# Layer 1's attention rebuilt: scores of four heads by 32 queries, 32x32 transposes on VectorE, sums on 32-row array tiles

## The chip, the core and the metric

The kernel runs on one core of one Trainium2 chip. Its time is the device time in microseconds (us) of one execution; the median of several is given. PE is TensorE's matmul side and PEld its weight loads, DVE is VectorE, ACT is ScalarE, POOL is GpSimd, SP is the engine that issues most DMAs. fp32 is used throughout; one fp32 matmul call of the program stands as two MATMUL instructions (with two weight loads) in the trace.

## The reference, cut to what matters

The program has four layers on x of shape (2, 256, 32, 32): two attentions over the image (layers 0 and 1), then a windowed attention with a mixture of experts, and an additive attention with a mixture of experts. The change touches layer 1 alone:

```
xn = groupnorm over the whole image (one mean, one variance), * gn_w + gn_b
q, k, v = w_in @ xn            # 8 heads of 64, N = 1024 positions
attn = softmax(q.T @ k / 8)    # per image and head, 1024 x 1024
out = attn @ v                 # 8 heads of 64 -> 512 channels
x = x + w_out @ out + b_out
```

For each of 2 images and 8 heads that is a 1024 x 1024 table of scores: 16 tables in all.

## The kernel before, in words

`run` calls `layer0`, then `layer1`, then turns `xT` (channels on partitions) into tokens, then the later layers. Nothing of the others is changed, but layer 0's `shared_attention` is of use as a source of durations: it makes scores on 64-row, 32-column tiles of the array (L261), turns most of its weights over with DVE transposes in 32x32 blocks (L311) and sums with 128-row, 64-column tiles (L337). Window attention makes its scores on 32-row, 64-column tiles (L752).

`layer1` first takes the statistics (L574 to L580, `pool_stats`, `rsqrt`), then works through 64 steps, written out by hand in `attention` under `manual_schedule`, so each engine runs its instructions in the order of the program. A step is one image, one pair of heads, 128 queries and all 1024 keys:

- `prepare` (only at the start of an image or a pair): `image` normalises on DVE (L594, L598) and makes the values (L607, copied out by ACT L611); `heads` makes this pair's queries and keys (L621, out by ACT L625).
- `score` (L132): four calls, two heads on the two 64-row halves of the array, into two PSUM tiles of 1024 columns. DVE copies each out with its minimum (L138); the scores carry a minus sign.
- `weigh` (L149): ACT's exp with the minimum as bias, and the row total.
- `turn` (L162): 16 transposes on PE into three PSUM buffers `ps_t`, copied out by ACT (L167, three of four) and DVE (L165).
- `invert`, `spread` (L180 to L190): the reciprocal of the total, spread along a row by POOL, turned by PE, copied by ACT.
- `value` (L199): 16 calls of 128 rows, 64 columns of the array; DVE multiplies the sums by the reciprocals into `oT` (L205). After an image's last step `output` (L634) projects and adds to `xT` on DVE (L640).

The stages lag behind each other: in step n PE runs score of n, the spread of n-3, turn of n-2 and the sums of n-3.

Of the kernel before, what the change touches and what calls it, by code (L numbers as in the profile page):

```python
# [27 lines left out]
P = 128  # L28
# [36 lines left out]
class Stack:  # L65
# [34 lines left out]

    def attention(self, rows, keys, pools):

        tc, nc = self.tc, self.nc
        p_s, p_t, p_o, sb = pools
        KB = 1024
        per = keys // KB
        lag = per + 1
        steps = [(i, j) for i in range(len(rows)) for j in range(per)]
        least, total, scores, weights, sums, norm = {}, {}, {}, {}, {}, {}

        def score(i, j):
            row = rows[i]
            if j == 0:
                row["prepare"]()
                least[i] = self.small.tile([P, 2, per], F32, name="least", tag=f"least{per}")
                total[i] = self.small.tile([P, 2, per], F32, name="total", tag=f"total{per}")
            q, k = row["q"](), row["k"](j)
            ps = [p_s.tile([P, KB], F32, name=f"ps_s{r}") for r in range(2)]
            for c in range(KB // CH):
                for r in range(2):  # L130
                    half = slice(64 * r, 64 * r + 64)
                    nc.tensor.matmul(  # L132
                        ps[r][:, c * CH : (c + 1) * CH], lhsT=q[half], rhs=k[half, c * CH : (c + 1) * CH],
                        start=True, stop=True,
                    )
            scores[i, j] = [sb.tile([P, KB], F32, name=f"sc{r}", bufs=lag + 1) for r in range(2)]
            for r in range(2):
                nc.vector.tensor_scalar(  # L138
                    scores[i, j][r], ps[r], 1.0, None, ALU.mult, ALU.min,
                    accum_out=least[i][:, r, j : j + 1],  # L140
                )
            if j == per - 1 and per > 1:
                m = self.small.tile([P, 2], F32, name="least1")
                nc.vector.tensor_reduce(m, least[i], AX.X, ALU.min)
                least[i] = m.unsqueeze(2)

        def weigh(i, j):
            for r in range(2):
                nc.scalar.activation(  # L149
                    scores[i, j][r], scores[i, j][r], AF.Exp, bias=least[i][:, r, 0:1], scale=-1.0,  # L150
                    accum_out=total[i][:, r, j : j + 1],
                )

        def turn(i, j):
            e = scores.pop((i, j))
            weights[i, j] = {}
            for c in range(KB // CH):
                for r in range(2):
                    ps = p_t.tile([P, CH // P, P], F32, name="ps_t")
                    for k in range(CH // P):  # L160
                        at = c * CH + k * P
                        nc.tensor.transpose(ps[:, k, :], e[r][:, at : at + P], self.ident)  # L162
                    w = sb.tile([P, CH // P, P], F32, name="wt", bufs=9)
                    if c == 1 and r == 1:
                        nc.vector.tensor_copy(w, ps)  # L165
                    else:
                        nc.scalar.copy(w, ps)  # L167
                    weights[i, j][r, c] = w

        def invert(i, j):  # L170

            if j < per - 1:
                return
            t = total.pop(i)
            if per > 1:
                d = self.small.tile([P, 2], F32, name="total1")
                nc.vector.tensor_reduce(d, t, AX.X, ALU.add)
                t = d.unsqueeze(2)
            rec = self.small.tile([P, 2, 1], F32, name="rec")
            nc.vector.reciprocal(rec, t)  # L180
            norm[i] = sb.tile([P, 2, 64], F32, name="wide", bufs=2)
            nc.gpsimd.tensor_copy(norm[i], rec.to_broadcast([P, 2, 64]))

        def spread(i, j):
            if j < per - 1:
                return
            ps = p_t.tile([P, CH // P, P], F32, name="ps_t")
            nc.tensor.transpose(ps[:, 0, :], norm[i].rearrange("p a b -> p (a b)"), self.ident)
            norm[i] = sb.tile([P, P], F32, name="norm", bufs=2)
            nc.scalar.copy(norm[i], ps[:, 0, :])  # L190

        def value(i, j):
            row, w = rows[i], weights.pop((i, j))
            if j == 0:
                sums[i] = p_o.tile([P, P], F32, name="ps_o")
            po = sums[i]
            for k in range(KB // P):
                for r in range(2):
                    nc.tensor.matmul(  # L199
                        po[64 * r : 64 * r + 64, :], lhsT=row["v"](r, j * (KB // P) + k),  # L200
                        rhs=w[r, k // (CH // P)][:, k % (CH // P), :],
                        start=(j == 0 and k == 0), stop=(j == per - 1 and k == KB // P - 1),
                    )
            if j == per - 1:
                nc.vector.tensor_tensor(row["o"](), sums.pop(i), norm.pop(i), ALU.mult)  # L205
                row["finish"]()

        with tc.manual_schedule():
            for n in range(len(steps) + lag + 1):
                at = lambda d: steps[n - d] if 0 <= n - d < len(steps) else None  # L210
                for stage, d in (
                    (invert, lag + 1), (score, 0), (spread, lag + 1), (turn, lag), (weigh, lag - 1), (value, lag + 1)
                ):
                    if at(d):
                        stage(*at(d))

    def attention_pools(self, ctx):
        pool = lambda name, bufs: ctx.enter_context(self.tc.tile_pool(name=name, bufs=bufs, space=PSUM))
        sb = ctx.enter_context(self.tc.tile_pool(name="att_sb", bufs=2))
        return pool("p_s", 1), pool("p_t", 3), pool("p_o", 1), sb  # L220
# [332 lines left out]
    def layer1(self, xT):  # L553
        tc, nc = self.tc, self.nc
        HEADS, HID = 8, 512
        with ExitStack() as ctx:
            w = ctx.enter_context(tc.tile_pool(name="l1_w", bufs=1))
            big = ctx.enter_context(tc.tile_pool(name="l1_big", bufs=1))
            qk = ctx.enter_context(tc.tile_pool(name="l1_qk", bufs=2))
# [3 lines left out]

            pools = self.attention_pools(ctx)
            p_r = pools[1]
# [19 lines left out]
            mean, var = self.pool_stats(w, p_r, mv, average, "ps_t")  # L585
            rs = self.rsqrt(var, 1e-5)
# [3 lines left out]
            def image(b):  # L590
                xn[b] = big.tile([P, CC, N], F32, name="xn", bufs=2)
                for c in range(CC):
                    j = c * B + b
                    nc.vector.tensor_scalar(  # L594
                        xn[b][:, c, :], xT[:, c, b * N : (b + 1) * N],
                        mean[:, j : j + 1], rs[:, j : j + 1], ALU.subtract, ALU.mult,
                    )
                    nc.vector.tensor_scalar(  # L598
                        xn[b][:, c, :], xn[b][:, c, :], gn_w[:, c : c + 1], gn_b[:, c : c + 1],
                        ALU.mult, ALU.add,  # L600
                    )
                v[b] = big.tile([P, N // P, HID], F32, name="v", bufs=2)
                oT[b] = big.tile([P, HID // P, N], F32, name="oT", bufs=2)
                for i in range(N // P):
                    ps = p_r.tile([P, HID], F32, name="ps_t")
                    for c in range(CC):
                        nc.tensor.matmul(  # L607
                            ps, lhsT=xn[b][:, c, i * P : (i + 1) * P], rhs=w_in[:, c, 2 * HID :],
                            start=(c == 0), stop=(c == CC - 1),
                        )  # L610
                    nc.scalar.copy(v[b][:, i, :], ps)  # L611

            def heads(b, pair):

                for part, to, scale in ((0, q, -0.125), (1, k, 1.0)):
                    to[b, pair] = qk.tile([P, N], F32, name="qh" if part == 0 else "kh")
                    for t in range(N // CH):
                        ps = p_r.tile([P, CH], F32, name="ps_t")
                        for c in range(CC):
# [22 lines left out]
            def row(b, pair, i):  # L642
                def prepare():
                    if pair == 0 and i == 0:
                        image(b)
                    if i == 0:
                        heads(b, pair)
# [936 lines left out]
```

## Time and profile before

| what | us |
|---|---|
| median of 3 runs (3086.73 to 3088.11) | 3087.94 |
| the profiled execution | 3088.63 |
| its span | 3086.9 |
| layer 0's steps, about | 60 to 1271 |
| layer 1, reciprocal of the deviation to last addition | 1286.8 to 1792.8 |
| first score of layer 1 / last score of layer 1, start | 1311.0 / 1759.1 |
| PE, DVE, ACT, POOL busy in the span | 2854.8, 1876.2, 1988.2, 447.3 |
| mean granted clock of TensorE | 0.962 |

Rows of groups read: line, engine, operation, output<-input, array rows*columns and shapes, count | busy us, mean ns of one | idle time of the engine just before, and what ended most of it. Rows in order of time read: start, duration, engine, line, operation; "x8" are eight instructions merged, whose duration runs from the first start to the last end, and the ends of matmuls are modelled, so the next instruction can start before. Rows by stage read: from:to, length, then busy time and number of instructions of PE, PEld, DVE, ACT, POOL, then the granted clock as a share of full speed, the DMA share and GB/s.

### The profile page before, as it was taken

What the parts mean: (1) busy time and instruction counts of PE and PEld (TensorE: products, weight loads), DVE (VectorE), ACT (ScalarE), POOL (GpSimd) and SP (SyncE); (2) the same over time, 40 slices, a digit from 0 to 9 for tenths busy, and PEclk for the clock granted to TensorE, in tenths of its full rate; (3) what the DMA queues carried; (4) which work ended last, traced back from release to release, by engine and by line L of the source; (5) the groups of instructions that cost most, each with busy time, mean ns of one, the idle gap of its engine ahead of it and who ended that gap; (6) DMA issues with size and microseconds to landing.
All of it is one profiled execution on the core that took longest, in us unless ns stands there. A gap on an engine that the chain in (4) does not pass through costs nothing.

```text
span 3086.9 us, 71663 instructions
## 1 busy us (share of the span) xinstructions
PE 2854.8 (92%) x29414; PEld 1844.6 (60%) x29414; DVE 1876.2 (61%) x3698; ACT 1988.2 (64%) x2977; POOL 447.3 (14%) x576
## 2 busy tenths in 40 slices
PE   7999999999999999899999978699799977997967
PEld 4466566666666666566566745598566633563656
DVE  5998989889898989445345467653422333223343
ACT  1887878788887878366556622121399776986811
POOL 3000000000000000000000023442311112223233
PEclk9999999999999999999999998799899988999988
DMA  3000000000000000000000010344222112222334
GB/s 125 3 3 3 3 3 3 3 3 3 3 3 3 3 3 3 29 1 1 1 1 1 2 26 1 127 141 150 94 77 75 40 33 74 80 75 73 117 109 150
DMA packets 179894, 126.83 MB, mean 41 GB/s; under 512 B 133152, under 2 KB 161456, under 8 KB 175216
## 3 DMA queue, kind: packets, MB, share of 16 engines
q0 software_dynamic: 36864, 85.93, 8.5%
q1 hardware_dynamic: 141264, 35.87, 5.2%
q8 instruction: 231, 3.78, 0.5%
q14 instruction: 95, 0.78, 0.1%
q10 hardware_dynamic: 1440, 0.47, 0.1%
HBM read 181.24 MB, written 29.49 MB: 68 GB/s over the span
## 4 chain that ended last, share of the span: by engine, by line
PE 84%; DVE 5%; issue 3%; DMA 3%; ACT 2%; POOL 2%; another core or an unknown queue 1%; SPq 0%; POOLq 0%; DVEq 0%; ACTq 0%
PE ps_s L261 15%; PE ps_o L337 15%; PE ps_h L1240 8%; PE ps_y L1254 8%; PE ps_e L1391 7%; PE ps_t L319 5%; PE ps_s L132 4%; PE ps_o L199 4%; PE ps_t L162 4%; PE ps_t L621 2%; PE ps_v L1428 2%; PE ps_out L516 1%; PE ps_qk L450 1%; PE ps_t L607 1%
## 5 line engine op out<-in xcount | busy, mean ns | idle before, releaser
L298 ACT ACTIVATE sc<-sc,sa_shift 128x1024 f32<-128x1024 f32 x512 | 585.1, 1148 | 56.7 <-DMA sa_shift<-sa_min 56.5
L1382 ACT ACTIVATE th<-kT,qb 128x1024 f32<-128x1024 f32 x512 | 542.1, 1135 | 114.2 <-PE ps_e L1391 75.3
L261 PE MATMUL ps_s<-kT,qT 64*32 64x512 f32 x8192 | 504.9, 596 | 9.3 <-ACT sc L271 8.9
L337 PE MATMUL ps_o<-wt,v 128*64 128x128 f32 x6144 | 503.2, 276 | 0.0
L337 PEld LDWEIGHTS ps_o<-wt,v 128*64 128x64 f32 x6144 | 442.1, 137 | 42.8 <-issue 42.8
L311 DVE STREAM_TRANSPOSE wt<-sc 128x768 f32<-128x768 f32 x512 | 465.7, 943 | 1.1 <-ACT sc L298 1.1
L271 ACT COPY sc<-ps_s 128x1024 f32<-128x1024 f32 x256 | 257.3, 1005 | 115.1 <-PE ps_s L261 43.2
L1240 PEld LDWEIGHTS ps_h<-xe,ew 128*128 128x128 f32 x2320 | 278.6, 195 | 62.1 <-issue 35.9
L282 DVE TENSOR_REDUCE sa_least<-sc 128x1 f32<-128x1024 f32 x256 | 306.1, 1196 | 2.5 <-ACT sc L271 2.4
L268 DVE TENSOR_SCALAR_CACHE_REDUCE sc<-ps_s 128x1024 f32<-128x1024 f32 x256 | 301.4, 1177 | 5.9 <-PE ps_s L261 5.9
L1240 PE MATMUL ps_h<-xe,ew 128*128 128x128 f32 x2320 | 293.4, 281 | 10.5 <-DVE xe L1219 8.8
L1391 PE MATMUL ps_e<-th,pick 128*32 128x512 f32 x2048 | 284.7, 619 | 19.7 <-DVE ir_half L955 14.2
L1254 PE MATMUL ps_y<-ew,h 128*128 128x256 f32 x1160 | 272.8, 384 | 8.0 <-issue 4.3
L138 DVE TENSOR_SCALAR_CACHE_REDUCE sc<-ps_s 128x1024 f32<-128x1024 f32 x128 | 151.8, 1222 | 180.2 <-PE ps_s L132 180.2
L337 PE MATMUL ps_o<-wl,v_odd 128*64 128x128 f32 x2048 | 251.9, 276 | 0.0
L1254 PEld LDWEIGHTS ps_y<-ew,h 128*128 128x128 f32 x1160 | 212.7, 190 | 64.5 <-issue 21.8
L261 PEld LDWEIGHTS ps_s<-kT,qT 64*32 64x32 f32 x8192 | 127.3, 106 | 200.7 <-issue 170.1
L1229 ACT ACTIVATE h<-hb 128x512 f32<-128x512 f32 x145 | 90.1, 623 | 243.5 <-DVE hb L1245 197.1
L1245 DVE TENSOR_TENSOR hb<-ps_h,ew 128x512 f32<-128x512 f32 x145 | 100.1, 690 | 240.0 <-PE ps_h L1240 202.0
L319 PEld LDWEIGHTS ps_t<-ident,sc 128*128 128x128 f32 x1024 | 107.8, 141 | 216.4 <-issue 172.0
L337 PEld LDWEIGHTS ps_o<-wl,v_odd 128*64 128x64 f32 x2048 | 221.2, 137 | 0.0
L348 POOL TENSOR_TENSOR diag<-ident,sa_rec 32x128 f32<-32x128 f32 x64 | 25.1, 391 | 1172.4 <-DVE sa_rec L345 1172.4
(266 smaller groups left out, 3660.4 us busy)
## 6 DMA issues: line engine op xcount, KB each, us to landing
xr<-slots_in SPq DMA_DIRECT2D x99, 128.0 KB
slots_out<-y SPq DMA_DIRECT2D x99, 128.0 KB
sa_got<-sa_least SPq DMA_DIRECT2D x512, 0.5 KB
sa_shift<-sa_min SPq DMA_DIRECT2D x512, 0.2 KB
slots_in<-zero POOLq DMA_DIRECT2D x46, 128.0 KB
sa_sums<-sa_total SPq DMA_DIRECT2D x256, 1.0 KB
xT<-in_x SPq DMA_DIRECT2D x4, 496.0 KB
ew<-in_l_up,rt_rows POOLq DMA_INDIRECT x99
```

Source lines behind the costliest of these rows:

```text
L261: nc.tensor.matmul(ps[r][S * c : S * (c + 1), a, :].rearrange("p (b i) -> p b i", i=S), lhsT=qT[half, p, S * i : S * (i + 1)], rhs=keys[ha ...
L268: nc.vector.tensor_scalar(scores[m][0], flat[0], 1.0, None, ALU.mult, ALU.min, accum_out=least[m // 2][:, 0, h : h + 1])
L271: nc.scalar.copy(scores[m][1], flat[1])
L282: nc.vector.tensor_reduce(least[m // 2][:, 1, h : h + 1], scores[m][1], AX.X, ALU.min)
L298: nc.scalar.activation(scores[m][r], scores[m][r], AF.Exp, bias=shift[m // 2][:, r : r + 1], scale=-1.0, accum_out=total[i][:, 2 * p + r, ...
L311: nc.vector.transpose(weights[i, h][:, 2 * p + r, :], scores[m][r][:, :DIRECT])
L319: nc.tensor.transpose(ps[:, g, r, :], s[:, at : at + P], self.ident)
L337: nc.tensor.matmul(sums[i][64 * k : 64 * (k + 1)], lhsT=values, rhs=w, start=(h == 0 and j == 0 and t == 0), stop=(h == 1 and j == 1 and t ...
L1240: nc.tensor.matmul(ps[:, j, :], lhsT=a[:, c, at : at + P], rhs=x[:, c, :], start=(c == 0), stop=(c == CC - 1),)
L1254: nc.tensor.matmul(ps, lhsT=h[:, j, :], rhs=w2[:, j, :], start=(j == 0), stop=(j == HB - 1))
L1382: nc.scalar.activation(h, keys, AF.Tanh, bias=self.qb[b][:, s // G, g : g + 1])
L1391: nc.tensor.matmul(pe[i][c * U : (c + 1) * U, a, :], lhsT=self.pick[:, k, :], rhs=h[:, a, :], start=(k == 0), stop=(k == G - 1),)
```

## The change

`attention` and `attention_pools` go; `layer1` gets a schedule of its own with 64 slots in place of the 64 steps:

- A slot (`score`) is four heads by two blocks of 32 queries by 1024 keys: 16 calls on 64-row, 32-column tiles, the four heads on the four column strips, a block of queries on each 64-row half. So that each head meets both halves, every projected query and key tile is stored twice, the second time with its two 64-row halves exchanged by two DMAs (`take` in `heads`).
- DVE copies out with the minimum as before; ACT's exp as before. The reciprocal now scales the weights themselves, on POOL (`share`).
- `turn` is one DVE transpose in 32x32 blocks of each 128 x 1024 tile; nothing goes through PE or PSUM.
- `value`, every second slot: 128 calls with 32 keys of one head (32 rows) by 64 columns, moving 4 x 32 queries; each head has a PSUM bank, the first and second half of the keys go to its lower and upper 64 partitions. `join` copies the upper half out on ACT, and DVE adds the two halves into `oT` (two additions).
- Projections, values and outputs are jobs, two in each odd slot that the table `jobs` names (17 with projections after slot 4, 6 with outputs, within the 64 slots). The values of image 0 are in slots 0 to 3. Jobs and sums share one PSUM buffer of four banks (tag `ps_r`, one buffer); scores have the other four.
- The group norm is folded into one scale and shift; image 1 is normalised on POOL after slot 18.

The diff, without the removed parts that the section above describes and without unchanged setup:

```
-            pools = self.attention_pools(ctx)
-            p_r = pools[1]
+            psum = lambda name: ctx.enter_context(tc.tile_pool(name=name, bufs=1, space=PSUM))
+            p_s, p_r = psum("l1_s"), psum("l1_r")
+            banks = lambda name: p_r.tile([P, H, CH], F32, name=name, tag="ps_r")
...
+            nc.vector.tensor_tensor(by_image(scale), by_image(scale), channel(gn_w), ALU.mult)
+            nc.vector.tensor_tensor(shift, mean, scale, ALU.mult)
+            nc.vector.tensor_tensor(by_image(shift), channel(gn_b), by_image(shift), ALU.subtract)
...
+            def heads(part, b, quad, p, half):
+                def job(ps):
...
+                    for c in range(CC):
+                        nc.tensor.matmul(
+                            ps, lhsT=w_in[:, c, at : at + P], rhs=xn[b][:, c, half * CH : (half + 1) * CH],
+                            start=(c == 0), stop=(c == CC - 1),
+                        )
+                    def take():
+                        nc.scalar.activation(to[:, 0, :], ps, AF.Copy, scale=(-0.125, 1.0)[part])
+                        for r in range(2):
+                            nc.sync.dma_start(
+                                out=to[64 * r : 64 * r + 64, 1, :], in_=to[64 - 64 * r : 128 - 64 * r, 0, :]
+                            )
+                    return take
+                return job
+            def values(b, n):
+                def job(ps):
...
+                    for a in range(4):
+                        at = (4 * n + a) * S
+                        for c in range(CC):
+                            for h in range(H):
+                                nc.tensor.matmul(
+                                    ps[S * h : S * (h + 1), a], lhsT=xn[b][:, c, at : at + S],
+                                    rhs=weights[:, c, h], start=(c == 0), stop=(c == CC - 1),
+                                )
+                    def take():
+                        for u in range(2):
+                            nc.scalar.copy(v[b][u][:, 4 * n : 4 * n + 4, :], ps[:, :, u, :])
+                    return take
+                return job
+            def output(b, n, o):
...
+                    return lambda: nc.vector.scalar_tensor_tensor(
+                        x, ps, b_out[:, o : o + 1], x, ALU.add, ALU.add
+                    )
...
+            jobs = {n: [values(0, 2 * n), values(0, 2 * n + 1)] for n in range(4)}
...
+                5: queries(0, 0, 1), 7: keys(0, 1, 0), 9: keys(0, 1, 1), 11: queries(0, 1, 0), 17: queries(0, 1, 1),
+                21: keys(1, 0, 0), 23: keys(1, 0, 1), 25: queries(1, 0, 0), 35: queries(1, 0, 1), 37: outs(0, 0),
+                39: keys(1, 1, 0), 41: keys(1, 1, 1), 43: outs(0, 1), 45: queries(1, 1, 0), 47: outs(0, 2),
+                49: outs(0, 3), 51: queries(1, 1, 1), 57: outs(1, 0), 61: outs(1, 1), 65: outs(1, 2), 67: outs(1, 3),
+            jobs.update({27 + 2 * n: [values(1, 2 * n), values(1, 2 * n + 1)] for n in range(4)})
+            def score(n):
...
+                            half, side, p = slice(64 * r, 64 * r + 64), (h + r) % 2, h // 2
+                            col = at % CH + S * r
+                                ps[r][S * h : S * (h + 1), a * CH : (a + 1) * CH],
+                                lhsT=x[half, side, p, col : col + S],
+                                rhs=y[half, side, p, a * CH : (a + 1) * CH], start=True, stop=True,
...
+            def weigh(n, r):
+                nc.scalar.activation(
+                    scores[n][r], scores[n][r], AF.Exp, bias=least[n][r], scale=-1.0, accum_out=total[n][r]
+                )
+            def share(n, r):
+                nc.vector.reciprocal(rec[n][r], total[n][r])
+                nc.gpsimd.tensor_scalar(scores[n][r], scores[n][r], rec[n][r], None, ALU.mult)
+            def turn(n, r):
+                if n % 2 == 0 and r == 0:
+                    turned[n // 2] = sb.tile([P, 4, N], F32, name="wt")
+                nc.vector.transpose(turned[n // 2][:, n % 2 * 2 + r, :], scores[n][r])
+            def value(m):
...
+                x, ps = turned.pop(m), banks("ps_o")
+                for t in range(BLOCKS // 2):
+                    for h in range(H):
+                        rows = slice(S * h, S * (h + 1))
+                        for j in range(2):
+                            at = BLOCKS // 2 * j + t
+                            nc.tensor.matmul(
+                                ps[64 * j : 64 * j + 64, h, :P], lhsT=v[b][quad][rows, at, :],
+                                rhs=x[rows, :, S * at : S * (at + 1)], start=(t == 0), stop=(t == BLOCKS // 2 - 1),
+                            )
+            def join(m):
...
+                nc.scalar.copy(other, ps[64:128, :, :P])
+                def add():
+                    for r in range(2):
+                        nc.vector.tensor_tensor(
+                            to[64 * r : 64 * r + 64], ps[0:64, r::2, :P], other[:, r::2, :], ALU.add
                         )
+                return add
+            image(0, nc.vector)
+            with tc.manual_schedule():
+                for n in range(0, len(first), 2):
+                    ps = banks("ps_j")
+                    for take in [job(ps[:, i, :]) for i, job in enumerate(first[n : n + 2])]:
+                        take()
+                for n in range(SLOTS + 4):
+                    on = lambda d: 0 <= n - d < SLOTS
+                    if on(2):
+                        turn(n - 2, 0)
+                    if on(1):
+                        share(n - 1, 1)
+                    if on(2):
+                        turn(n - 2, 1)
+                    copies = score(n) if on(0) else []
+                    add = join((n - 5) // 2) if n % 2 == 1 and on(5) else None
+                    for copy in copies:
+                        copy()
+                    if add:
+                        add()
+                    if on(0):
+                        weigh(n, 0)
+                    takes = []
+                    if n % 2 == 0 and on(4):
+                        value((n - 4) // 2)
+                    elif n in jobs:
+                        ps = banks("ps_j")
+                        takes = [job(ps[:, i, :]) for i, job in enumerate(jobs[n])]
+                        takes.pop(0)()
+                    if on(0):
+                        share(n, 0)
+                        weigh(n, 1)
+                    for take in takes:
+                        take()
+                    if n == NORM:
+                        image(1, nc.gpsimd)
```

## The prediction, on record before the result

> **What bounds the kernel now.** I read the busy times by stage first, then one step of layer 1 in order of time, then the rows elsewhere in this trace that have the shapes the change brings in. Layer 1 runs from the group-norm scale (reciprocal at 1286.8 us) to its last addition into `xT` (ends 1792.8): 506 us of the 3086.9 us span. A steady stretch of it:
>
> ```profile
> core 0: us, PE busy (x) PEld busy (x) DVE busy (x) ACT busy (x) POOL busy (x), PEclk, DMA share, GB/s
> 1400.00:1500.00 100.00, 100.00 (x861) 67.82 (x863) 49.39 (x103) 64.44 (x127) 4.45 (x15) 1.00 0.01 1
> ```
>
> PE has no idle time and full clock; DVE is half empty. One step (two heads, 128 queries, 1024 keys) in order of time:
>
> ```profile
> 1424.42 1.99 PE L132 MATMUL ps_s<-kh,qh 64*128 64x512 f32 x8
> ...
> 1426.34 0.33 PE L188 MATMUL ps_t<-ident,wide 128*128 128x128 f32 x1
> ...
> 1426.44 1.22 DVE L138 TENSOR_SCALAR_CACHE_REDUCE sc<-ps_s 128x1024 f32<-128x1024 f32 x1 [1.47 <-PE ps_s L132]
> 1426.51 1.93 PE L162 MATMUL ps_t<-ident,sc 128*128 128x128 f32 x16
> ...
> 1428.37 1.97 PE L199 MATMUL ps_o<-wt,v 128*64 128x128 f32 x32
> ...
> 1430.26 1.99 PE L132 MATMUL ps_s<-kh,qh 64*128 64x512 f32 x8
> ```
>
> Score to score is 5.84 us, all PE: 1.92 score, 0.17 spread, 1.86 turning, 1.89 sums. 64 steps are 374 us; projections and outputs (per image 15.4 for the values, 4 x 7.06 for heads, 14 out) add 115. First score ends 1313, last 1761.1.
>
> **What the change removes and adds.** Turning and spreading (2.03 x 64 = 130 us of PE) go. DVE gets two 1024-wide transposes per slot, POOL two scalings, ACT loses the PSUM copies. Rows for the new forms:
>
> ```profile
> L311 DVE STREAM_TRANSPOSE wt<-sc 128x768 f32<-128x768 f32 x512 | 465.7, 943 | 1.1 <-ACT sc L298 1.1
> ```
> ```profile
> 699.77 1.95 PE L261 MATMUL ps_s<-kT,qT 64*32 64x512 f32 x32
> 701.64 0.66 PE L319 MATMUL ps_t<-ident,sc 128*128 128x128 f32 x4
> ```
> ```profile
> 1877.26 0.49 PE L752 MATMUL ps_s<-kh,qh 32*64 32x64 f32 x32
> 1877.67 0.33 PE L789 MATMUL ps_pt<-ident,probs 128*128 128x128 f32 x1
> ```
>
> - *Score* is layer 0's form exactly (16 calls, eight 64*32 tiles): 1.87 us to the next instruction, 2.0 to its last result.
> - *Sums*: 128 calls of 32*64 x 128 columns are 256 instructions on eight tiles. A 128-column instruction takes 0.107 us of one tile (L337: 16 rounds in 1.71, 1.90 with the change of form). If the eight overlap, 32 rounds are 3.4, with 0.2 for the change of form **3.6 us** per two slots. L752 shows eight 32*64 tiles overlapping: 32 instructions in 0.41 us, 13 ns each, where 13.4 are needed. Bounds: 3.4, and 6.9 if only four of the eight run together. I take 3.6.
> - The Trainium skill, "TensorE: Matmul & The Clock Gate", Part 1, speaks against this: it says that start to start never drops below about 25 ns however small the matmul is. By it the sums would be 256 x 25 ns = 6.4 us and layer 1 some 90 us longer (an estimate from that page). This trace has 13 ns, so I follow the trace.
> - *DVE*: two copies with minimum 2 x 1.15 (L138, start to start); two transposes of 1024. Pairs of 768 start 0.89 apart, so 1.16 each (between 0.89 and 0.89 x 4/3 = 1.19); two reciprocals 0.13; every second slot two additions of 256 columns, 0.4 each (L816 has 0.42). Even slot 5.15 us, odd 5.95.
> - *POOL*: 128x1024, one input. Nearest rows: L484 copies 512 columns in 0.86, L770 multiplies 512 in 1.04, a 1024 memset is 0.95. So 0.95 to 2.1 each, two per slot, with a whole slot of slack before the transposes: nothing. It would count from 2.7 each.
> - *ACT*: two exps 2.4, one 0.6 copy per two slots, 1.2 to 1.5 for a pair of jobs: under 4.6 per slot, covered.
> - *DMAs*: each of the 32 jobs for heads adds two of 128 KB on SP's queue, which is empty in layer 1 (1 GB/s in the first row above); the slots that read them come three to eleven slots, 17 us or more, later. Nothing but at the start (below). Image 1 is normalised on POOL in slot 18 in two operations of 0.95 to 2.1; first read in slot 21: nothing.
> - *Instructions*: layer 1's PE stream grows some three times; the instruction queue's packets stand at 231 for the whole program. I take nothing; a late packet of 16 KB would cost part of a microsecond.
>
> **The slot.** One PSUM buffer of four banks (`ps_r`) serves sums and jobs in turn, and that sets the order. Let a slot begin when its score's last result is there (T).
> Even slot: sums follow at once, then the next score: 3.6 + 1.87 = **5.5**; DVE's 5.15 fits under it.
> Odd slot without jobs: the next score waits only for the two copies; DVE's 5.95 is late. DVE then carries the pair: with some overlap at the seams 10.8 for two slots.
> Odd slot with jobs (projections): PE stands until DVE has made its two copies (2.3) and both additions (3.1), since the jobs write the banks that the additions read; then two jobs 3.6 (L621: 7.06 for four), then the score 2.0: **8.8**. ACT's second exp waits behind the first job's take, which makes DVE ready at about 8.4: equal, not later.
> Odd slot with outputs: their additions are on DVE, in front of a reciprocal and two transposes: 9.8, less 0.3 regained in the next slot.
> Of the 63 steps from score 0 to score 63: the first five 5.5; then 17 pairs with projection jobs at 14.3, 6 with outputs at 15.0, 6 without at 10.8: 27.5 + 243 + 90 + 65 = **425 us**.
> *Start*: normalising takes DVE 1.6 instead of 3.2 and three small steps more (0.6); PE begins at 1288.6, at half clock until 1292.0 as before; three pairs of projections at 4.4 (one buffer, so the takes are not hidden) end 1303.3. Then the halves of keys and queries are swapped by DMA: 256 KB behind the last takes; the stage 1262 to 1282 moved 77 GB/s at least, so under 3.4 us, plus landing: score 0 ends 1308.5, before 1313.
> *End*: from the last score, sums and outputs alternate through one buffer: 3.2 + 3.6 + 2.1 + 4.1 + 3.6 + 1.8 + 4.1 = 22.5; before, 31.7.
> Sum at full clock: 1308.5 + 425 + 22.5 = 1756, that is **36 us earlier** than 1792.8.
>
> **The clock.** In every odd slot with jobs PE streams nothing for 3.2 us and the 0.15 us that the last score's tail takes: 3.35. Before, layer 1 had no such gap. What such gaps do here is seen in stretches of 3.41 us laid on the instants at which the granted clock changes:
>
> ```profile
> 1254.14:1257.56 3.42, 0.44 (x10) 0.20 (x4) 2.37 (x4) 2.68 (x5) 0.00 (x0) 1.00 0.01 0
> 1257.56:1260.97 3.41, 3.20 (x24) 2.87 (x26) 0.70 (x1) 2.90 (x6) 0.00 (x0) 0.50 0.00 0
> 1520.38:1523.79 3.41, 2.01 (x4) 0.79 (x5) 2.37 (x4) 0.00 (x0) 0.17 (x1) 1.00 0.00 0
> 1523.79:1527.20 3.41, 3.41 (x9) 1.52 (x8) 0.00 (x0) 1.17 (x2) 0.00 (x0) 1.00 0.00 0
> 1882.19:1885.61 3.42, 1.56 (x21) 1.18 (x12) 2.66 (x11) 2.32 (x5) 0.56 (x1) 1.00 0.00 0
> 1885.61:1889.02 3.41, 3.41 (x42) 2.53 (x41) 1.41 (x5) 0.12 (x1) 2.24 (x3) 0.50 0.00 0
> ```
>
> A stretch with PE busy 0.44 or 1.56 us is followed by one at clock 0.50, one with 2.01 is not. So about 2 us idle within a stretch is enough. A gap of 3.35 puts 2 us into some stretch if that begins within 3.35 + 3.41 - 4 = 2.75 of 3.41: 8 gaps in 10. The half-speed stretch then falls on the jobs and the score, which are what the slot waits for: 1.7 us lost, 1.8 with the cases where a second stretch follows. 23 slots x 0.8 x 1.8 = 33; slots after outputs, with gaps a microsecond longer, 3; slots without jobs, where PE has a microsecond in hand, 2; start and end 4. **42 us lost** (bounds: 0, and one stretch in each of 31 odd slots and the ends, 60).
> The same page's rule, § HAM oscillation, that gaps under about 3.4 us are safe would leave nothing of this 42 and give 36 us of gain; the row with 1.56 busy speaks against it.
>
> **Sum.** -36 + 42 = +6 on the profiled execution's 3088.63 (its span 3086.9 and 1.7 around it); the median shown is 0.7 lower, 3087.94. Forecast **3094 us**: the work saved on PE comes back as waiting for the one buffer and as half clock. Own range 3072 to 3116 (clock loss 20 to 64).
>
> **Rivals.**
> 1. *The clock holds*: slots fall so that few stretches have 2 us idle, or half speed falls where DVE is late anyway. For it: 6 of 29 pairs are DVE's. Against: the rows above. 3088 - 36 = **3052** (3040 to 3070).
> 2. *The sums on 32-row tiles do not overlap eightfold* at 128 columns, since each row strip gets 64 weight loads in 3.4 us. L752 is 32 instructions long and shows a burst only. Price: every us beyond 3.6 is paid 32 times, at once in the 23 job pairs. At 4.6 us +32, at 6.9 us +106: 3125 to **3200**. It decides from 3.9 us on.
> 3. *DVE is the bound in every slot* (transposes slower beside POOL): 6.0 per slot only equals today's 5.84, and job pairs have 3 us in hand; +0 to 20, within the forecast's range.
>
> **Chances.** Forecast 0.50, clock holds 0.25, sums slow 0.18, anything else 0.07. Range 3046 to 3145 leaves out part of rivals 1 and 2. This kernel's times can tell 0.2%, 6 us, from no change: faster 0.25 + 0.13 of the forecast's half = 0.38; same 0.14; slower 0.48.
>
> **What would show it.** Sums: groups of 256 matmuls in 3.6 us. Odd job slots: PE idle 3.2 us, ended by DVE's addition. Clock in layer 1 near 0.8 instead of 1.00; if it stays over 0.95, rival 1. Score to score 5.5 and 8.8. Last score near 1773. Wrong if POOL's scaling takes over 2.7 us, or PE waits on transposes.

## The result and the profile after

| what | before | after |
|---|---|---|
| median of 4 runs, us | 3088.03 (3086.73 to 3090.00) | 3173.58 (3168.01 to 3178.53) |
| ratio, 95% interval | | 1.0276 (1.0254 to 1.0298) |
| the profiled execution / its span | 3088.63 / 3086.9 | 3178.53 / 3176.8 |
| mean granted clock of TensorE | 0.962 | 0.945 |
| first result complete / start of last score | 1313 / 1759.1 | 1311.7 / 1848.5 |
| last addition of layer 1 ends | 1792.8 | 1881.1 |
| half clock between 1330 and 1870 us | 15.1, none of it in layer 1 | 112.6 |
| half clock from the first score's result to the last score's end | 13.7 | 109.2 |
| PE instructions in layer 1 / packets of the instruction queue | 7994 / 31 | 23111 / 91 |

Half clock is the time in which TensorE's granted clock stood at 0.50 of full speed.

The change makes the kernel 2.8% slower: 3173.6 against a forecast of 3094 and a range to 3145. Layer 1 ends 88 us later, which is nearly all of the 90 us that the span grew. The line numbers below are those of the changed kernel: score L591, copy with minimum L602, exp L609, scaling on POOL L615, turning on DVE L620, sums L631, other half by ACT L644, additions L648, projection jobs L509, L536 and L553.

The same stage that was read before, by stage, same columns (PE, PEld, DVE, ACT, POOL busy, then the clock):

```profile
1400.00:1500.00 100.00, 72.70 (x1977) 36.65 (x1977) 66.17 (x116) 37.16 (x63) 73.76 (x29) 0.91 0.08 18
```

PE had no idle time and now has 27 us in 100, and its clock is 0.91 where it was 1.00. Where the idle time is, PE's rows in order of time show:

```profile
1405.22 3.67 PE L509 MATMUL ps_j<-xn,sb_l_w_in 128*128 128x512 f32 x8 [3.38 <-DVE oT L648]
1408.82 1.95 PE L591 MATMUL ps_s<-kh,qh 64*32 64x512 f32 x32
1411.19 2.61 PE L631 MATMUL ps_o<-wt,v 32*64 32x128 f32 x163 [0.42 <-ACT qh L515]
1415.21 1.62 PE L631 MATMUL ps_o<-wt,v 32*64 32x128 f32 x93 [1.41 <-issue]
1416.77 1.95 PE L591 MATMUL ps_s<-kh,qh 64*32 64x512 f32 x32
1420.09 3.09 PE L591 MATMUL ps_s<-kh,qh 64*32 64x512 f32 x32 [1.38 <-DVE sc L602]
1423.11 3.48 PE L631 MATMUL ps_o<-wt,v 32*64 32x128 f32 x227
1427.68 0.69 PE L631 MATMUL ps_o<-wt,v 32*64 32x128 f32 x29 [1.08 <-issue]
```

The gap of 3.38 us ahead of the jobs, ended by DVE's addition, is the one that was predicted. The breaks inside the sums (163 and then 93, 227 and then 29) were not: one group of 256 MATMUL instructions runs at 14 ns each, stops once, and goes on. The label "issue" says that PE waited for nothing that the profile shows. The groups of instructions say what it adds up to:

```profile
L631 PE MATMUL ps_o<-wt,v 32*64 32x128 f32 x8192 | 137.1, 275 | 49.6 <-issue 40.4 <-ACT qh L515 3.0 <-ACT v L543 2.8
L509 PE MATMUL ps_j<-xn,sb_l_w_in 128*128 128x512 f32 x128 | 85.2, 828 | 48.0 <-DVE oT L648 39.6 <-DVE l_rec L614 3.5 <-ACT kh L515 2.5
L615 POOL TENSOR_SCALAR sc<-sc,l_rec 128x1024 f32<-128x1024 f32 x128 | 362.6, 2844 | 218.3 <-DVE l_rec L614 218.3
L620 DVE STREAM_TRANSPOSE wt<-sc 128x1024 f32<-128x1024 f32 x128 | 155.3, 1225 | 2.2 <-POOL sc L615 2.2
L489 POOL TENSOR_SCALAR xn<-xT,rs_r,gn_shift 128x1024 f32<-128x1024 f32 x2 | 2.4, 1188 | 0.0
```

A group of sums takes 5.55 us in the mean (3.87 to 7.39), not 3.6. POOL's scaling takes 2.84 us, over the bound of 2.7 that the prediction gave, though a row of the same shape with two operations (L489) takes 1.19; the turning hardly waits for it (2.2 us in all).

The clock, in stretches of 3.41 us laid on its changes, around the gap of slot 5 (score ends at 1343.43):

```profile
1342.28:1345.69 3.41, 1.15 (x24) 0.15 (x8) 2.17 (x3) 0.84 (x1) 3.07 (x2) 1.00 0.00 0
1345.69:1349.10 3.41, 2.30 (x3) 1.18 (x4) 2.26 (x6) 0.40 (x2) 2.16 (x1) 0.50 0.00 0
1349.10:1352.52 3.42, 3.42 (x5) 1.35 (x4) 0.00 (x0) 0.00 (x0) 0.69 (x1) 0.50 0.00 0
```
```profile
1341.48 1.95 PE L591 MATMUL ps_s<-kh,qh 64*32 64x512 f32 x32
1346.80 6.51 PE L509 MATMUL ps_j<-xn,sb_l_w_in 128*128 128x512 f32 x8 [3.37 <-DVE oT L648]
```

PE is idle 2.3 us in the first, and the two that follow, in which the jobs run, stand at half. That slot, from the end of its score to the end of the next, takes 11.8 us; one with no half clock takes 8.9.

**Theories.** Theory A for the stops: PE is out of instructions. The 74480 instructions of PE, its weight loads and its sequencer in this trace come with 291 packets of 16 KB of the instruction queue, that is 256 to a packet. All 30 stops inside the sums lie at the same place of this stream, the first instruction after a whole multiple of 256 (counted from the program's start, less 193), and end 1.25 to 1.60 us after a packet has landed. Three of them, a stop counted from the start of the instruction before it to the start of the next, which is 0.26 us more than the idle time in brackets above:

```
PE stops  multiple of 256 passed before   packet from .. to     PE goes on
1339.02   1337.17                         1337.99 .. 1339.00    1340.39
1413.54   1411.69                         1412.30 .. 1413.75    1415.21
1426.33   1424.50                         1425.32 .. 1426.28    1427.68
```

From one multiple to the next PE needs 2.9 to 4.1 us (median 3.4) where it stops, whereas 256 instructions (128 matmuls with their weight loads) run in 1.8. A group of sums is 512. In the two groups without a stop PE lost about 0.8 us at the same place of the stream in the score that follows. Theory B, the prediction's second rival: the eight 32-row tiles do not overlap over a long group. Theory C for the rest: the gap ahead of the jobs is paid as a wait and again as half clock. Against it: the clock follows the amount of work, or POOL and DVE are next in line and take whatever is freed.

### The profile page after: what moved, and what is told of

The parts are those of the page before. It is cut to its first block, busy times and chain, and to the rows that moved or that the text cites. A ratio compares the mean times of both kernels' runs of the same rounds, so it can differ in the third digit from the quotient of the medians.

```text
span 3176.8 us, 86798 instructions
## 1 busy us (share of the span) xinstructions
PE 2800.2 (88%) x37030; PEld 1777.0 (56%) x37030; DVE 1992.8 (63%) x3831; ACT 1894.6 (60%) x2769; POOL 789.4 (25%) x642
## 5 line engine op out<-in xcount | busy, mean ns | idle before, releaser
L615 POOL TENSOR_SCALAR sc<-sc,l_rec 128x1024 f32<-128x1024 f32 x128 | 362.6, 2844 | 218.3 <-DVE l_rec L614 218.3
L147 DVE TENSOR_SCALAR_CACHE_REDUCE sc<-ps_s 128x1024 f32<-128x1024 f32 x256 | 301.4, 1177 | 6.4 <-PE ps_s L140 6.4
L1418 PE MATMUL ps_e<-th,pick 128*32 128x512 f32 x2048 | 286.3, 628 | 21.6 <-DVE ir_half L982 14.3
L609 ACT ACTIVATE sc<-sc,l_least 128x1024 f32<-128x1024 f32 x128 | 146.8, 1148 | 213.9 <-DVE sc L602 211.3
```

The costliest lines, as they stand in the source:

```text
L147: nc.vector.tensor_scalar(scores[m][0], flat[0], 1.0, None, ALU.mult, ALU.min, accum_out=least[m // 2][:, 0, h : h + 1])
L615: nc.gpsimd.tensor_scalar(scores[n][r], scores[n][r], rec[n][r], None, ALU.mult)
L1418: nc.tensor.matmul(pe[i][c * U : (c + 1) * U, a, :], lhsT=self.pick[:, k, :], rhs=h[:, a, :], start=(k == 0), stop=(k == G - 1),)
```

## The experiments

The runs went to several chips, on which before takes 3062 to 3089 us, so each is compared with before on its own chip. The changed kernel itself, run again:

**after_same_chip.** No edit.

> The changed kernel, unedited, on the chip of the other runs, to compare the single looks with: ratio to before 1.0276 as at first, so about 3147 us where before takes 3062; sums 5.5 us in the mean, stops at every 256 PE instructions, half clock between first and last score 100 to 125 us.

Measured: 3181.4 where before takes 3089.2, ratio 1.0305 (1.0289 to 1.0320); it landed on a chip like the first, so the factor, about 1.029, is what carries over: where before takes 3062, the changed kernel would take about 3151 (worked out, not run). Half clock between 1330 and 1870 us 109 us; pairs of slots with projection jobs 19.07 us where the first trace has 19.04.

**half_rounds.** Leaves out half of the sums.

```diff
-                for t in range(BLOCKS // 2):
+                for t in range(BLOCKS // 4):
...
```

> Leaves out half of the sums: 8 of the 16 rounds of blocks, so 128 matmuls (256 PE instructions with their weight loads) per two slots instead of 256 (512). Theory A, PE is out of instructions in the middle of each group of sums: in the changed kernel every stop lies on a multiple of 256 PE instructions and ends 1.3 to 1.5 us after a packet of the instruction queue has landed; with 256 instructions a group holds one such place, the one for which the packet had time, so the group takes 1.8 to 2.0 us with no stop, at the same 13.4 ns. Theory B, the 32-row tiles do not run together eightfold over a long group: 2.8 us, half of 5.55. The whole run 50 to 90 us below the changed kernel by either; the row decides.

Measured: 3088.3 us (one run; before 3061.9), 63 below the 3151. PE's rows:

```profile
1403.81 2.15 PE L631 MATMUL ps_o<-wt,v 32*64 32x128 f32 x128 [0.42 <-ACT qh L515]
1405.88 2.99 PE L591 MATMUL ps_s<-kh,qh 64*32 64x512 f32 x32
```
```profile
L631 PE MATMUL ps_o<-wt,v 32*64 32x128 f32 x4096 | 69.7, 277 | 9.4 <-ACT qh L515 3.0 <-ACT v L543 2.8 <-ACT kh L515 2.5
```

No stop in any group, and the 40.4 us of "issue" are gone: 2.1 us for 128 matmuls, a little over theory A's 2.0 and well under theory B's 2.8. It also shows that not every us of the sums is paid: 3.4 us less per group, 32 times, is 108, and 63 came back. In an even slot PE then waits for DVE's copies, and job slots without half clock grow from 8.9 to 9.5 us, since DVE is behind when they begin: the gap ahead of the jobs is 3.9 us there, not 3.4.

**narrow_sums.** Leaves out half of the sums in the other direction.

```diff
-                                ps[64 * j : 64 * j + 64, h, :P], lhsT=v[b][quad][rows, at, :],
-                                rhs=x[rows, :, S * at : S * (at + 1)],
+                                ps[64 * j : 64 * j + 64, h, : P // 2], lhsT=v[b][quad][rows, at, :],
+                                rhs=x[rows, 0:2, S * at : S * (at + 1)],
...
```

> Leaves out half of the sums in the other direction: all 256 matmuls (512 PE instructions) per two slots, each over 64 queries instead of 128; the output's other queries are filled with copies. Theory A (instructions): from one multiple of 256 instructions to the next PE needs 3.2 to 3.5 us whatever the matmuls are, so a group takes 3.3 + 0.9 = 4.2 us, its stop grows from 1.6 to about 2.4 us. Theory B (tiles, work by columns): 2.8 us, half of 5.55, with a stop no longer than before. Theory B2 (a price per instruction, no stop): 5.5 us.

Measured: 3169.0 (one run; before 3061.9). A group in order of time:

```profile
1427.85 2.63 PE L631 MATMUL ps_o<-wt,v 32*64 32x64 f32 x227
1432.24 0.48 PE L631 MATMUL ps_o<-wt,v 32*64 32x64 f32 x29 [1.76 <-issue]
```

With half of the columns a group still takes 5.29 us; the stop grows from 1.61 to 2.12 us in the mean, as A has it, and from one multiple of 256 to the next it is 3.6 us in the median, where it was 3.4. So the work is not what the group waits for, which ends theory B. The group's length alone is near B2's 5.5, but B2 has no stop, and between the stops a matmul takes 11 ns. The 4.2 us were a miss: a matmul of 64 columns takes 11 ns and not 7, so the running part shrank by 0.75 us and not by 1.7. Nor is the run shorter than the 3151, for half clock grew from 109 to 178 us between the first and the last score; why was not followed up. The two kernels together: half of the instructions removes the stop, half of the columns does not.

**add_first.** One edit of the order on VectorE.

```diff
-                    for copy in copies:
-                        copy()
                     if add:
                         add()
+                    for copy in copies:
+                        copy()
```

> One edit: in odd slots the additions stand ahead of the two copies on VectorE. Theory C (the gap in front of the jobs brings the half clock): additions end with or before the score, jobs follow the score at once, PE idle ahead of L509 falls from 3.4 us to under 1; half clock in layer 1 falls from 127 us to under 40; job slots go from 8.9 to 11.8 us to 5.6 to 6.5, the 23 pairs with jobs from about 18 to 13.5: the run about 3060 us. Rival (the clock follows the work, not the gap): half clock stays over 100 us and only the wait goes: 3173 - 23 x 3.2 = about 3100. Rival (GpSimd's scaling at 2 x 2.84 per slot, or VectorE, is next in line and takes the gain): over 3120.

Measured: 3043.9 where before takes 3061.9, ratio 0.9928 (0.9904 to 0.9952): the order alone turns 2.8% slower into 0.7% faster. One pair of slots:

```profile
1349.09 3.83 PE L631 MATMUL ps_o<-wt,v 32*64 32x128 f32 x253 [0.42 <-ACT qh L515]
1354.44 0.43 PE L631 MATMUL ps_o<-wt,v 32*64 32x128 f32 x3 [1.52 <-issue]
1354.80 1.95 PE L591 MATMUL ps_s<-kh,qh 64*32 64x512 f32 x32
1356.68 3.70 PE L509 MATMUL ps_j<-xn,sb_l_w_in 128*128 128x512 f32 x8
1360.31 1.95 PE L591 MATMUL ps_s<-kh,qh 64*32 64x512 f32 x32
```

The jobs follow the score at once. ACT copies the other half and DVE adds while the score runs, and the copies, which the jobs do not need, run beside the jobs. Pairs with projections go from 19.04 to 14.04 us, with outputs from 17.97 to 13.29; half clock from the first score's result to the last score's end goes from 109 to 28 us (between 1330 and 1870 us, which here reaches 99 us past layer 1, from 113 to 51; in layer 1 it is 42, a little over the 40 expected). The stop stays.

**add_middle.** The additions between the two copies.

```diff
-                    for copy in copies:
+                    for copy in copies[:1]:
                         copy()
                     if add:
                         add()
+                    for copy in copies[1:]:
+                        copy()
```

> One edit: in odd slots the additions stand between the two copies on VectorE. PE's gap ahead of the jobs falls from 3.4 us to about 2.1. Theory C with the prediction's measure (2 us idle within a stretch of 3.41 us brings the next stretch to half): hardly any job slot is hit, half clock between the first and the last score falls from 113 us to under 40, job slots without half clock 7.8 us, the run about 23 x (1.15 + 1.9) = 70 us below the changed kernel, ratio to before near 1.005. If gaps of 2 us are as bad as gaps of 3.4: half clock stays near 100 us, the run 26 us below.

Measured: 3128.8 (one run; before 3062.8), 23 us below the 3151: the second case, not mine.

```profile
1343.88:1347.29 3.41, 1.18 (x17) 0.30 (x2) 2.49 (x5) 1.21 (x2) 2.84 (x2) 1.00 0.00 0
1347.29:1350.71 3.42, 3.42 (x5) 1.35 (x4) 1.94 (x4) 0.03 (x1) 2.53 (x1) 0.50 0.00 0
```
```profile
1346.89 5.37 PE L509 MATMUL ps_j<-xn,sb_l_w_in 128*128 128x512 f32 x8 [2.23 <-DVE oT L648]
```

A gap of 2.23 us still brings half clock to 20 of the 23 pairs with jobs (106 us in all), only one stretch of it instead of sometimes two. ("Hardly any" did not follow even from the prediction's own formula, by which a gap of 2.1 us puts 2 us into some stretch in 4 cases of 10.) Over the stretches of layer 1 at full clock, in all eleven traces, those with PE busy under 1.3 us were always followed by half, those with 2.15 or more never, and between the outcome was mixed. So idle time of about 1.5 us in a stretch can be enough, where the prediction took 2. In add_first this was:

```profile
1396.80:1400.21 3.41, 1.93 (x26) 0.32 (x18) 2.77 (x7) 1.37 (x3) 2.35 (x1) 1.00 0.03 7
1400.21:1403.62 3.41, 3.41 (x38) 0.78 (x30) 2.55 (x5) 1.02 (x2) 3.24 (x2) 0.50 0.00 0
```

**warm_gap.** Adds work whose result is not used.

```diff
...
+                        if add:
+                            for i in range(26):
+                                nc.tensor.matmul(
+                                    joined[:, 0, CH - P :], lhsT=whole, rhs=whole, start=True, stop=True,
+                                )
                         ps = banks("ps_j")
```

> Adds work: in each odd slot with jobs from slot 5 on, 26 matmuls of 128 columns whose result is not used stand between the score and the jobs, 26 x 0.107 = 2.8 us in a gap of 3.4. The order and the waits stay. Theory C (the gap brings the half clock): half clock in layer 1 falls from 127 us to under 40, job slots go back to 8.9 us, the run is 40 to 55 us shorter, about 3125, though PE does more. Rival (the clock follows the amount of work, or something else than idle time): half clock stays or grows, the run is at 3173 or above.

Measured: 3303.3, ratio to before 1.0790 (1.077 to 1.081), 5% above the changed kernel. It did not test what it was made for:

```profile
1475.22 6.04 PE L683 MATMUL ps_o<-whole 128*128 128x128 f32 x52 [3.37 <-DVE oT L648]
1481.33 3.70 PE L509 MATMUL ps_j<-xn,sb_l_w_in 128*128 128x512 f32 x8
```

The matmuls write a column range that nobody reads, but it lies in the tile that the additions read, and so they waited for the additions as the jobs do; and an fp32 matmul is two instructions, so they last 6.0 us. What it still says: the gap of 3.4 us stands, and so does the half clock, in 20 of the 23 pairs with jobs, with more work on PE; and 25 slots x 6.04 = 151 us were paid in full (152 above the 3151), so in a job slot nothing covers PE.

**pool_forms.** The scaling in four forms, for even and odd slots and the two tiles of a slot.

```diff
...
+ nc.gpsimd.tensor_scalar(scores[n][r], scores[n][r], rec[n][r], zero, ALU.mult, ALU.add)
+ nc.gpsimd.tensor_scalar(to, scores[n][r], rec[n][r], None, ALU.mult)
+ nc.gpsimd.tensor_scalar(to, scores[n][r], rec[n][r], zero, ALU.mult, ALU.add)
```

> GpSimd's 128 scalings in four forms, 32 of each: as in the changed kernel (one operation, in place), two operations in place (times the scalar, plus a zero tile, the form of the normalising row that takes 1.19 us), one operation into another tile, two operations into another tile. If the form makes the 2.84 us against 1.19, the two rows with two operations take 1.2; if being in place makes it, the two rows with another tile do; if sharing with VectorE's work makes it, all four stay near 2.84. Time: theory, GpSimd is off the path (VectorE waits for it 2.2 us in all), so within 0.3% of the changed kernel whatever the rows say; rival, GpSimd at 5.7 us per slot paces the pairs, and a faster form takes 10 us or more off.

Measured: 3138.6 (one run; before 3062.8), 12 us or 0.4% below the 3151. By the marks set beforehand (0.3%, 10 us) that is on the rival's side. But job slots without half clock take 8.93 us as before; what is less is half clock, 72 us against 109 from the first score's result to the last score's end. Whether the form does that one run cannot say; add_first_two_op, below, asks again.

```profile
L618 POOL TENSOR_SCALAR sc<-sc,l_rec 128x1024 f32<-128x1024 f32 x32 | 90.9, 2841 | 105.8 <-DVE l_rec L616 105.8
L623 POOL TENSOR_SCALAR sh<-sc,l_rec 128x1024 f32<-128x1024 f32 x32 | 90.9, 2840 | 127.0 <-DVE l_rec L616 127.0
L627 POOL TENSOR_SCALAR sh<-sc,l_rec,zero 128x1024 f32<-128x1024 f32 x32 | 38.4, 1200 | 69.4 <-DVE l_rec L616 69.4
L620 POOL TENSOR_SCALAR sc<-sc,l_rec,zero 128x1024 f32<-128x1024 f32 x32 | 38.4, 1200 | 0.2 <-POOL sc L618 0.2
```

The form is all of it: with a second operation that does nothing the scaling takes 1.20 us instead of 2.84, in place or not.

**split_sums.** Ten of the 16 rounds of the sums before the next score, six behind it, and the additions between the copies.

```diff
...
                     copies = score(n) if on(0) else []
+                    if n % 2 == 1 and on(5):
+                        value((n - 5) // 2, range(10, 16))
...
-                        value((n - 4) // 2)
+                        value((n - 4) // 2, range(10))
```

> 10 of the 16 rounds of the sums stay in the even slot, 6 come behind the next score, so that a score (64 PE instructions in 1.9 us) stands between 320 and 192 instructions of sums; the additions stand between the two copies. Theory A (a refill each 256 instructions that can't be passed sooner than 3.2 us after the one before): stops shrink from 1.6 us to under 0.5; 2.5 and 1.5 us for the two parts; even slot 4.5, odd slot with jobs 8.7, pairs 13.2 where the changed kernel has 16.8 to 19.8; PE's gap ahead of the jobs 1.4 us, so the clock holds; the run near 3060, ratio to before near 0.99. Theory B (tiles do not overlap): the parts take 3.4 and 2.1, pairs 15, ratio above 1.005.

Measured: 3056.3 where before takes 3062.8, ratio 0.9980 (0.9970 to 0.9989).

```profile
1350.01 2.54 PE L633 MATMUL ps_o<-wt,v 32*64 32x128 f32 x160 [0.42 <-ACT qh L515]
1352.48 2.60 PE L591 MATMUL ps_s<-kh,qh 64*32 64x512 f32 x32
1355.01 1.65 PE L633 MATMUL ps_o<-wt,v 32*64 32x128 f32 x96
1358.31 3.67 PE L509 MATMUL ps_j<-xn,sb_l_w_in 128*128 128x512 f32 x8 [1.64 <-DVE oT L648]
1361.91 1.95 PE L591 MATMUL ps_s<-kh,qh 64*32 64x512 f32 x32
```

The parts take 2.5 and 1.65 us, nearly the 2.5 and 1.5 of theory A, though a score still lost 0.65 us in the middle here (2.60 for 1.95). This pair is 14.3 us (14.7 in the mean of the 17), not 13.2. From the end of one score to the end of the next, the odd slot takes 8.8 us, as expected; the even one takes 5.5 and not 4.5, for the 0.42 us ahead of the sums and the 0.65 in the score. Half clock fell to 17 us from the first score's result to the last score's end, and none of it lies in the 17 pairs with projections, though each has a gap of 1.64 to 1.72 us.

The kernel that differs from this one in the split alone is add_middle, on the same chip:

```profile
L631 PE MATMUL ps_o<-wt,v 32*64 32x128 f32 x8192 | 137.9, 277 | 51.4 <-issue 39.9 <-ACT qh L515 3.0 <-ACT v L543 2.8
L633 PE MATMUL ps_o<-wt,v 32*64 32x128 f32 x8192 | 138.3, 276 | 18.3 <-issue 7.3 <-ACT qh L515 3.0 <-ACT v L543 2.8
```

With the same matmuls, "issue" ahead of the sums falls from 39.9 to 7.3 us and the run from 3128.8 to 3056.3. Of these 72 us some 40 are half clock (96 to 17 us from the first score's result to the last score's end). So the stop is paid, at once and through the clock; how much of the clock belongs to it and how much to the gap, which went from 2.23 to 1.7 us, is not shown.

**add_first_two_op.** add_first, with the second operation on POOL, the zero tile as above.

> add_first with GpSimd's scaling in two operations (times the scalar, plus a zero tile), which took 1.20 us against 2.84. Theory (the pairs with jobs are PE's, GpSimd is off the path): pairs with jobs stay at 13.5 us; the last slot's two scalings, which lie in the tail, give 3 us and the pairs without jobs a few tenths each: 3 to 8 us below add_first, ratio to before 0.990 to 0.992. Rival (GpSimd's 5.7 us per slot paces add_first, since its two in a row leave 13.5 - 11.4 only): 20 us or more below, ratio under 0.987.

Measured: 3063.6 where before takes 3089.2, ratio 0.9915 (0.9901 to 0.9928). POOL's busy time in the scaling falls from 362 to 153 us and DVE's wait for it from 2.4 to nothing; the pairs with jobs stay (14.2 and 12.9). The interval overlaps that of add_first, so the faster form is worth nothing that could be measured, and POOL was off the path. add_first and this one are the fastest versions run, 0.7 to 0.9% below before.

## Why the prediction was wrong, point by point

Layer 1 was forecast to end at 1756 + 42 = 1798 and ended at 1881.1, 83 us later. Pairs are taken from the end of one odd slot's score to that of the next odd one; "without half" is the mean of the pairs that had no half clock: 3 of the 17, 1 of the 6, and 3 of the 6. What a row has above that is put down to the clock.

| term | predicted | measured without half | measured | difference |
|---|---|---|---|---|
| first score complete | 1308.5 | | 1311.7 | +3.2 |
| first five slots | 27.5 | | 31.7 | +4.2 |
| 17 pairs with projections | 14.3 each | 16.8 each | 323.6 | +43, and clock 37.5 |
| 6 pairs with outputs | 15.0 each | 15.8 each | 107.8 | +5, and clock 13 |
| 6 pairs without jobs | 10.8 each | 11.6 each | 75.6 | +5, and clock 6 |
| from the last score to the end | 22.5 | | 30.6 | +8.1 |
| clock, a term of its own | 42 | | 56.5 in the pairs | +14.5 |

The sum of the differences is 3.2 + 4.2 + 43 + 5 + 5 + 8.1 + 14.5 = 83.

1. **The step that failed** is "*Instructions*: ... I take nothing; a late packet of 16 KB would cost part of a microsecond". It saw that the stream triples and looked at packets per program (231), not at how fast one group of sums eats them: 512 instructions in 3.8 us, two packets, where PE needed 3.4 us from one multiple of 256 to the next. Every group but two paid 1.0 to 2.2 us. That makes 5.55 us of the 3.6, and is most of the 2.5 us that a pair with projections is too long; another 0.42 is the wait for ACT's copy of the job ahead of the sums, which the prediction left out.
2. **Sums at 3.6 for eight tiles together** were nearly right for what they claimed: the two groups that had their packet in time took 3.87 and 4.02. The page weighed against them in the prediction (the Trainium skill, "TensorE: Matmul & The Clock Gate", Part 1), with 25 ns from start to start, does not describe matmuls on eight tiles of the array (14 ns here), though with the stops a group comes to 22 ns a matmul. Rival 2's price came near (it decides from 3.9, and 32 x 1.95 = 62 would give about 3156), but by luck, since its mechanism was another; narrow_sums ended that.
3. **The clock** was predicted with the right mechanism and sign, and a little too small: 56.5 us in the pairs against 42, within its bounds of 0 and 60. 19 of the 23 job slots between scores were hit, the 8 in 10 that were predicted, but eight of them by two stretches, which cost 2.9 us and not 1.8; and the slots without jobs lost 6 us where 2 were allowed. The measure of 2 us idle was too high, as add_middle showed, so that the share came out near is partly luck. Before's own trace had a case against it, in layer 1, ahead of 13.7 us at half:

```profile
1312.17:1315.58 3.41, 2.07 (x8) 0.41 (x6) 2.38 (x4) 2.13 (x4) 0.00 (x0) 1.00 0.00 0
1315.58:1319.00 3.42, 3.42 (x7) 1.19 (x8) 1.23 (x2) 1.10 (x2) 0.00 (x0) 0.50 0.00 0
```

4. **Job slots** at 8.8 without half clock: 8.9. The gap of 3.2 us, ended by DVE's addition: 3.4. Right.
5. **Slots without jobs** (10.8 a pair): 11.6. The DVE bound was near right: DVE is busy for 10.4 us of the 11.6, and half_rounds, with no stop and half of the sums, takes 10.7. That the rest is the stop fits, but is not shown.
6. **POOL's scaling as nothing, unless from 2.7 us**: it took 2.84, and was nearly nothing all the same, by 2.2 us of waiting. The bound from copies and multiplications was too low for the form with one operation.
7. **Start**: 3.2 us late; the swap of the queries by DMA let the score go on only at 1307.98, and then it ran at half clock until 1311.56, which the 4 us for start and end were to cover. **End**: 8.1 us late, with two stops, half clock and the same gaps.
8. **Was the loss in the design?** No. The prediction took the copies ahead of the additions as given; add_first shows what that order cost: layer 1 ends at 1771.1 there, 110 us before the changed kernel and 22 before the kernel before (on another chip, where layer 1's first matmul started 0.6 us earlier). The wait was named in the prediction ("PE stands until DVE has made its two copies (2.3) and both additions (3.1)"), but not asked whether it need be.

The Trainium skill, "Runtime: NRT & Kernel Launch", § Instruction fetch mechanics, says that an engine's instructions come in blocks of 16 KiB, 256 instructions, and that the cost of crossing a block is mostly hidden. The blocks are what these traces show; hidden they are not where PE runs 512 instructions in under 4 us: 1.6 us per crossing here. The page "TensorE: Matmul & The Clock Gate", § HAM oscillation, gives about 3.4 us as the gap that must not be exceeded; here add_middle's gaps of 2.23 us were enough, in 20 of 23 pairs of slots with jobs.

## What to carry to other kernels

Count instructions per stretch of time, not per program: many small matmuls (weight loads count) in one burst can be out of instructions, which shows as a break labelled "issue" at every 256th instruction, and fewer matmuls (half_rounds) or a slower operation in between (split_sums) avoid it. Where a gap on PE is forecast, ask which instruction in front of the releaser PE does not need, and move that behind it: the gap is paid once as a wait and again as half clock on what follows. And a gap has to be short, not only shorter, before the half clock goes: in this kernel gaps of 2.23 us ahead of the jobs brought it nearly every time, with gaps of 1.7 us in split_sums 1 of the 23 job slots had it.

## What the runs showed of the hardware that was not expected

- PE's instructions arrived in packets of 16 KB, 256 at a time. Inside the sums a packet started 0.6 to 1.7 us after the multiple of 256 before it, took 0.9 to 1.7, and PE went on 1.25 to 1.6 us after it had landed: 3.4 us in the median, 1.6 us of it a stop. After a quieter stretch the next packet was there already and the first multiple in a group cost nothing.
- A scaling of 128 x 1024 on GpSimd by one scalar per row took 2.84 us as one operation and 1.20 us as two.
- Matmuls on eight 32-row, 64-column tiles ran at 14 ns each with 128 columns and at 11 ns with 64.
- All changes of the granted clock in layer 1 lay on one grid of 3.413 us within a run, and idle time of about 1.5 us in one stretch could be enough to halve the next, while 2.1 us always was.
